# A fixed order for TensorE and the transfer queue in the opening of a one-layer decoder kernel

## The chip, the cores and the metric

The kernel runs on one core of one Trainium2 chip. The metric is the device time of one execution in microseconds (us); lower is better. Three runs of the kernel before took 2656.65, 2659.69 and 2660.51 us, with a median of 2659.69. All arithmetic is in float32.

## What is computed

A decoder layer on `x` of shape (4, 2048, 512). Three branches are each applied to a layer norm and added back to `x`:

```python
x = x + attn(_layernorm(x))          # a recurrence along the first axis (4 steps), 8 blocks of 64 states
x = x + xattn(_layernorm(x), ctx)    # 16 heads over 77 context rows
x = x + ffn(_layernorm(x))

# attn: z <- V (A z + u_t), output 2 Re z
# xattn: softmax(Q K^T / sqrt(32)) V, then Wo
# ffn:
h = einsum('bsd,dh->bsh', x, W_exp) + b_exp      # 512 -> 2048
h = butterfly(h, up_weights, 2048)               # 11 stages of 2x2 mixes
h = gelu(h + up_bias)
h = butterfly(h, down_weights, 2048)
y = einsum('bsh,hd->bsd', h, W_con) + b_con      # 2048 -> 512
```

The recurrence runs over only 4 steps, so it equals four 64 x 64 coefficient matrices. A butterfly is a linear map, so each of the two can be multiplied into the matrix beside it once, before any token is touched.

## The kernel before, in words

The program has an opening and sixteen equal units. A unit takes 128 positions of all four rows of the first axis. For unit u, `front` makes the recurrence, the norms and the cross attention, and `feed_forward` the third branch; `feed_forward(u)` draws `front(u + 1)` forward step by step, so that the two are mixed on TensorE. Products of two by two blocks use seven multiplications in place of eight (`seven`, and the seven matrices `up7`, `dn7`, `wq7`).

The opening prepares what the units need:

- `_recurrence_taps` (L68): the coefficients `gt`. A chain of small VectorE operations (L54 to L107), then four rounds of small products on TensorE (`ps_g` L111 and L112, `ps_rr` and `ps_ri` L121 to L124), each of which needs the VectorE results of the round before (L127 to L130).
- `_keys_values` (L134): loads the context and two weight matrices, then four groups of key products (L145), whose results are copied into the block-diagonal `kbd` by VectorE (L149), and four of value products (L154).
- `_prepare` (L218): multiplies the butterflies into the weights. For the first one: coefficient products on GpSimd (L179, L204), a bias product (L267), products over the low stages (L276), transposes (L285), products over the high stages against diagonals `bd` that VectorE makes (L242, L298, with the bias in L303), then for each of eight blocks four sums (L317 to L320, GpSimd and VectorE in turn) and stores to `up7`. For the second one: coefficient products on GpSimd (L179 on `low_dn`), products over the high stages (L333), transposes (L343), products over the low stages (L352), sums (L363 to L366) and stores to `dn7`.
- `front(0)`: the first unit's own front, with transposes L468 and L439, recurrence products L498, q products L483 (`ps_q`), scores L541, softmax L545 to L551, L563 to L575 and the output product L483 (`ps_w`).

These four are Python generators or plain calls; the code of L757 to L805 draws them forward. `next(prep)` issues the instructions up to the next `yield`. The order in which the code is written is however not the order on the chip: a scheduler that assigns the instructions to their engines reorders each engine's instructions by priority and by what is ready in its own estimate, except those held with `keep_in_program_order`. Each engine then takes its instructions strictly in the order so fixed, with semaphores between the engines. All transfers are issued by SP, one queue. Tiles come from pools with tags; a tile waits for a buffer of its tag to be free. The PSUM tag "f" has two buffers and serves the front and the recurrence; "a", "b" and "c" have two each and serve `_prepare`, keys and values.

In the opening's order before, the recurrence's products come between those of L276, keys and values come after the four groups of L298, and `front(0)` is mixed in from L468 on. The eight blocks of sums run beside keys and values. The last steps before unit 0's `feed_forward` are the seven `ps_w` products, a norm (L404 to L417, L430), the transposes L439, and then the first `ps_a` of L642, which needs the tile `w_up` that L651 loads. The tile `db` (L804), a bias, takes a buffer with the tag "xn", the one of the normalised rows of L430.

Of the kernel before, what the change touches and what calls it, by code (L numbers as in the profile page):

```python
# [17 lines left out]
P = 128  # L18
# [49 lines left out]
def _recurrence_taps(nc, pool, psum, ssm_vec, ssm_vt, ssm_vinv, gt):  # L68
# [40 lines left out]
    for j in range(T):  # L109
# [3 lines left out]
        for h in range(2):  # L113
            if j + h < T:
                q = slice(h * NS, (h + 1) * NS)
                nc.vector.tensor_scalar(gt[q, j + h, :], ps[q, 0:NS], 2.0, None, ALU.mult)
        if j == T - 1:
            break
# [15 lines left out]
def _keys_values(nc, psum, ctx_t, wk_t, wv_t, kbd, vsb, room):  # L134
# [82 lines left out]

def _prepare(nc, keep, pool, sums, room, banks, dram, ident, wexp_t, up_low, up_high, up_bias, dn_low, dn_high, wcon, wup, wdn, bias,  # L218
             up7, dn7):
# [19 lines left out]

    def diagonal(hp, m):  # L240
        bd = pool.tile([P, NB, sub], F32, tag="bd", bufs=4, name="bd")
        keep(nc.vector.tensor_tensor(bd, hp[:, m, :].unsqueeze(2).to_broadcast([P, NB, sub]),  # L242
                                     mask.unsqueeze(1).to_broadcast([P, NB, sub]), ALU.mult))
        return bd.rearrange("p b i -> p (b i)")
# [24 lines left out]
    nc.sync.dma_start(out=bias, in_=up_bias)  # L269
    mid = wup.rearrange("p c (m k) -> p c m k", m=NB)  # L270
    for g in range(4):
# [21 lines left out]
    for g in range(4):  # L293
        bd = [diagonal(hp, 4 * g + j) for j in range(4)]
        for c in range(NC):
# [78 lines left out]
def kernel(ctx: ExitStack, tc: tile.TileContext, x, ctx_t, ssm_vec, ssm_vt, ssm_vinv, wq_t, wk_t, wv_t,  # L374
# [381 lines left out]
    ready = []  # L756
    with ExitStack() as stack:  # L757
        pool = stack.enter_context(tc.tile_pool(name="prep", bufs=1))
        wup = pool.tile([P, NC, HID], F32, name="wup")
        wdn = pool.tile([P, NB, D], F32, name="wdn")  # L760
        with tc.tile_pool(name="taps", bufs=1) as taps:
            _recurrence_taps(nc, taps, psum, ssm_vec, ssm_vt, ssm_vinv, gt)
        sums = stack.enter_context(tc.tile_pool(name="sums", bufs=2))
        high = work.tile([P, 2, HIGH, NB // 2, 4], F32, tag="xn", name="high")
        prep = _prepare(nc, tc.keep_in_program_order, pool, sums, high, banks, dram, ident, wexp_t, up_low, up_high, up_bias, dn_low, dn_high, wcon,
                        wup, wdn, hbias, up7, dn7)
        next(prep)
        xts[0] = load_x(0)
        room = (work.tile([P, NC, T * NK], F32, tag="pr", name="ct"), xpool.tile([P, NC, D], F32, tag="xt1", name="wk"),
                work.tile([P, NC, D], F32, tag="qt", bufs=1, name="wv"))  # L770
        keys = _keys_values(nc, psum, ctx_t, wk_t, wv_t, kbd, vsb, room)
        next(keys)
        for _ in range(5):
            next(prep)
        wq = work.tile([P, 7, NC // 2, D // 2], F32, tag="pt", bufs=1, name="wq")
        first = front(0, xts.pop(0), ready, wq)
        for n, _ in enumerate(prep):
            for _ in range(1 + (n > 8)):
                next(first, None)
            if n == 7:  # L780
                next(keys)
                src = wq_t.rearrange("(c p) e -> p c e", p=P)
                for i, (c, e) in ((0, (0, 0)), (1, (1, 0)), (3, (1, 1)), (6, (0, 1))):
                    nc.sync.dma_start(out=wq[:, i], in_=src[:, 2 * c : 2 * c + 2, e * (D // 2) : (e + 1) * (D // 2)])
                tc.keep_in_program_order(nc.gpsimd.tensor_tensor(wq[:, 4], wq[:, 6], wq[:, 3], ALU.add))
                nc.gpsimd.tensor_tensor(wq[:, 6], wq[:, 0], wq[:, 6], ALU.subtract)
                nc.gpsimd.tensor_tensor(wq[:, 5], wq[:, 4], wq[:, 0], ALU.subtract)
                nc.gpsimd.tensor_tensor(wq[:, 2], wq[:, 1], wq[:, 5], ALU.subtract)
            if n == 9:
                nc.sync.dma_start(out=wq7, in_=wq)  # L790
            if n == 11:
                src = wo_t.rearrange("(c p) e -> p c e", p=P)
# [91 lines left out]
```

## Time and profile before

| | us |
|---|---|
| median of three runs | 2659.69 |
| the profiled execution | 2664.3 |
| its span, first to last instruction | 2662.5 |
| TensorE busy over the span | 2583.4 (97%) |
| VectorE, ScalarE, GpSimd busy | 1463.9, 807.3, 949.9 |
| TensorE busy in 0 to 249 us | 195.15 |
| first product of L642 starts | 248.96 |

A line of the timeline gives the start and the length in us, the engine, the line of the program, the operation, the tile written and those read, the shape, and how many instructions were merged into it; in brackets, the idle time before it and what ended that. A float32 product appears as two records. The line numbers are those of the kernel before; those of the same statement in the changed kernel are a few higher (seven from `front` on).

### The profile page before, as it was taken

The numbers are of one execution on the slowest core, as the hardware profiler recorded it, in microseconds if no ns is written. First come the engines' busy times: TensorE is split into PE (matmuls) and PEld (weight loads), VectorE is DVE, ScalarE is ACT, GpSimd is POOL, SyncE is SP. The second block draws the span as 40 slices with busy tenths as digits, with TensorE's granted clock in tenths as the row PEclk, the third lists the DMA queues.
The fourth block names the chain that finished last, engine by engine and source line by source line (L and its number), as shares of the span: only waits on it lengthen the run. The fifth ranks groups of instructions, "written<-read, shape, count | busy, mean of one in ns | idle before, by whom it ended". The sixth has DMA issues, their size and how long they took to land.

```text
span 2662.5 us, 37405 instructions
## 1 busy us (share of the span) xinstructions
PE 2583.4 (97%) x14536; PEld 2196.8 (83%) x14536; DVE 1463.9 (55%) x3350; ACT 807.3 (30%) x1466; POOL 949.9 (36%) x1023
## 2 busy tenths in 40 slices
PE   7887999999999999999999999999999999999999
PEld 6665888888888888888888888888888888888888
DVE  5567554556455455546555555655555564554541
ACT  2132413324141332414133241413234141423420
POOL 3323251523434152333415243341524234252523
PEclk9998999999999999999999999999999999999999
DMA  7704324242332424233342424333242423323243
GB/s 211 237 19 167 131 86 148 96 167 95 123 131 102 148 80 172 94 129 121 105 145 97 155 94 155 111 105 131 97 161 88 161 101 114 136 98 137 95 130 140
DMA packets 94656, 333.60 MB, mean 125 GB/s; under 512 B 17424, under 2 KB 46224, under 8 KB 77328
## 3 DMA queue, kind: packets, MB, share of 16 engines
q1 hardware_dynamic: 94480, 331.21, 35.7%
q8 instruction: 116, 1.90, 0.3%
q14 instruction: 60, 0.49, 0.1%
HBM read 297.61 MB, written 33.57 MB: 124 GB/s over the span
## 4 chain that ended last, share of the span: by engine, by line
PE 86%; DVE 7%; ACT 5%; issue 2%; POOL 0%; DMA 0%; SPq 0%; ACTq 0%; DVEq 0%; POOLq 0%
PE ps_a L709 13%; PE ps_b L642 10%; PE ps_b L709 8%; PE ps_q L483 7%; PE ps_w L483 7%; PE ps_c L642 7%; PE ps_a L642 7%; PE ps_c L709 6%; PE ps_sc L541 5%; PE ps_pt L563 4%; PE ps_s L498 3%; PE ps_o L573 2%; PE ps_t L439 2%; ACT L547 1%; ACT L647 1%
## 5 line engine op out<-in xcount | busy, mean ns | idle before, releaser
L642 PE MATMUL ps_b<-tb,w_up 128*128 128x256 f32 x1536 | 396.8, 379 | 1.2 <-DVE u L659 1.2
L709 PE MATMUL ps_a<-w_dn,a 128*128 128x256 f32 x1536 | 373.0, 380 | 0.0
L685 POOL TENSOR_TENSOR s<-a,a 128x256 f32<-128x256 f32 x128 | 92.7, 724 | 670.3 <-ACT a L647 447.9
L642 PEld LDWEIGHTS ps_b<-tb,w_up 128*128 128x128 f32 x1536 | 287.0, 190 | 40.9 <-issue 1.6
L647 ACT ACTIVATE a<-a,hbias 128x256 f32<-128x256 f32 x384 | 193.6, 508 | 410.9 <-DVE a L680 278.5
L709 PEld LDWEIGHTS ps_a<-w_dn,a 128*128 128x128 f32 x1536 | 282.4, 190 | 41.6 <-issue 3.0
L642 PE MATMUL ps_a<-xnt,w_up 128*128 128x256 f32 x1024 | 263.9, 381 | 0.0
L709 PE MATMUL ps_c<-w_dn,s 128*128 128x256 f32 x1024 | 248.6, 379 | 0.0
L551 POOL TENSOR_TENSOR pr<-pr,sm 128x1232 f32<-128x1232 f32 x64 | 143.9, 2248 | 288.8 <-DVE sm L550 241.0
L440 ACT COPY xnt<-ps_t 128x512 f32<-128x512 f32 x128 | 73.5, 586 | 550.7 <-PE ps_t L439 550.7
L642 PEld LDWEIGHTS ps_a<-xnt,w_up 128*128 128x128 f32 x1024 | 192.0, 191 | 25.7
L709 PEld LDWEIGHTS ps_c<-w_dn,s 128*128 128x128 f32 x1024 | 188.7, 190 | 27.8
L591 DVE TENSOR_TENSOR xt<-ps_w,xt 128x512 f32<-128x512 f32 x96 | 66.2, 689 | 215.0 <-PE ps_w L483 148.5
L697 POOL TENSOR_TENSOR xt<-xt,ybias 128x256 f32<-128x256 f32 x128 | 99.5, 811 | 223.2 <-DVE xn L430 223.2
L541 PE MATMUL ps_sc<-kbd,qt 128*128 128x308 f32 x512 | 173.5, 435 | 3.7 <-DVE pr L546 2.1
L483 PE MATMUL ps_q<-xnt,wq 128*128 128x256 f32 x640 | 152.4, 381 | 0.7 <-ACT qt L523 0.7
L563 PEld LDWEIGHTS ps_pt<-ident,pr 128*77 128x77 f32 x1024 | 117.9, 147 | 40.6 <-ACT a L647 11.0
L563 PE MATMUL ps_pt<-ident,pr 128*77 128x128 f32 x1024 | 143.8, 276 | 5.5 <-ACT a L647 4.7
L547 ACT ACTIVATE pr<-pr 128x308 f32<-128x308 f32 x256 | 111.5, 457 | 118.5 <-DVE pr L546 117.9
L483 PEld LDWEIGHTS ps_q<-xnt,wq 128*128 128x128 f32 x640 | 122.1, 191 | 17.9 <-ACT qt L523 1.1
L642 PE MATMUL ps_c<-tb,w_up 128*128 128x256 f32 x512 | 131.6, 379 | 0.0
L642 PE MATMUL ps_c<-xnt,w_up 128*128 128x256 f32 x512 | 131.5, 379 | 0.0
(199 smaller groups left out, 4550.8 us busy)
## 6 DMA issues: line engine op xcount, KB each, us to landing
w_up<-up SPq DMA_DIRECT2D x128, 896.0 KB, 4.5
w_dn<-dn SPq DMA_DIRECT2D x112, 1024.0 KB, 4.8
wq<-wq SPq DMA_DIRECT2D x16, 1792.0 KB, 8.5
xt<-in_x SPq DMA_DIRECT2D x16, 1024.0 KB, 5.4
out<-xt SPq DMA_DIRECT2D x64, 256.0 KB, 4.8
wdn<-in_wexp_t SPq DMA_DIRECT2D x4, 1024.0 KB, 11.3
wdn<-in_wcon SPq DMA_DIRECT2D x4, 1024.0 KB, 5.9
up<-s SPq DMA_DIRECT2D x8, 512.0 KB, 3.3
```

The lines of the kernel that those rows point to most:

```text
L440: nc.scalar.copy(xnt[:, :, t, :], ps)
L483: nc.tensor.matmul(tiles[key][:, r, :], lhsT=lhs(i, r, k), rhs=rhs(i, r, k), start=key == i and r == 0 and k == 0, stop=k == 1, skip_group ...
L498: nc.tensor.matmul(ps[:, 2 * i : T, f * NS : (f + 1) * NS], lhsT=xpt[:, i, c * (P // NS) + f, :], rhs=gt[:, 0 : T - 2 * i, :], start=i == ...
L541: nc.tensor.matmul(ps[:, 0 : 4 * NK], lhsT=qt[:, g, t, :], rhs=kbd[:, t, g, :], start=True, stop=True)
L547: nc.scalar.activation(pg, pg, AF.Exp, scale=1.0 / math.sqrt(DH))
L551: nc.gpsimd.tensor_tensor(pr, pr, sm.unsqueeze(2).to_broadcast([P, NH, NK]), ALU.mult)
L563: nc.tensor.transpose(pt_ps[0:NK, j, :], pr[:, 4 * g + j, :], ident)
L642: nc.tensor.matmul(ps, lhsT=w[:, c, :], rhs=rhs[i - 1][:, c], start=first and c == 0, stop=c == 1, skip_group_check=True)
L647: nc.scalar.activation(out, x, AF.Gelu, bias=hbias[:, b : b + 1])
L685: nc.gpsimd.tensor_tensor(s1, a21, a22, ALU.add)
L697: nc.gpsimd.tensor_tensor(r, r, ybias[:, d], ALU.add)
L709: nc.tensor.matmul(ps[:, t, :], lhsT=act[p][lhs[i]][:, t, :], rhs=w[:, p, :], start=first and p == 0 and t == 0, stop=p == h - 1, skip_gro ...
```

## The change

In the opening the order of TensorE and of SP is no longer left to the scheduler: under `manual_schedule` they take their instructions as the code writes them. VectorE, ScalarE and GpSimd are still scheduled. The code that draws the generators forward is rewritten: the recurrence now yields after each round, keys and values after each group, and the steps are interleaved by the list of `run` calls. By it the load of x comes first; keys and values stand between the recurrence's rounds; the first half of `front(0)` comes before L276; the high coefficients are loaded ahead of the low ones; q, scores and softmax stand between the groups of L298 and the sums, `ps_w` between the steps of L343 and L352; the second unit's x (`load_x(1)`) is loaded last. To that end the sums and the diagonals use the tiles of `wo`, `ybias` and a new `more` as room in place of pool buffers, the weights `wcon` are loaded by quarters after each group of L298, and the bias product takes the bias as its stationary operand, with one row as its result.

```diff
@@ _recurrence_taps
                 nc.vector.tensor_scalar(gt[q, j + h, :], ps[q, 0:NS], 2.0, None, ALU.mult)
+        yield
         if j == T - 1:
             break
@@ _keys_values
     for g in range(NC):
-        ps = psum.tile([P, 512], F32, tag="a", name="ps_k")
+        ps = psum.tile([P, 512], F32, tag="ab"[g % 2], name="ps_k")
...
                                   ps[q, 0 : T * NK].rearrange("p (b k) -> p b k", b=T))
+        yield
     for b in range(T):
-        ps = psum.tile([P, 512], F32, tag="b", name="ps_v")
+        ps = psum.tile([P, 512], F32, tag="c", name="ps_v")
...
         nc.scalar.copy(vsb[:, b, :], ps[0:NK, :])
-    yield
+        yield
@@ _prepare
-    def diagonal(hp, m):
-        bd = pool.tile([P, NB, sub], F32, tag="bd", bufs=4, name="bd")
+    def diagonal(hp, m, place):
+        bd = place.rearrange("p (b i) -> p b i", b=NB)
...
+    brw = room2
+    for high, coefs in zip(highs, (up_high, dn_high)):
+        nc.sync.dma_start(out=high, in_=coefs)
...
-    for high, coefs in zip(highs, (up_high, dn_high)):
-        nc.sync.dma_start(out=high, in_=coefs)
     yield
...
-    ps = banks()
-    for b in range(NB):
-        nc.tensor.matmul(ps[:, b : b + 1], lhsT=e[:, b, :], rhs=b1[:, b : b + 1], start=True, stop=True)
-    nc.vector.tensor_copy(b1, ps[:, 0:NB])
+    for g in range(4):
+        ps = banks()
+        for j in range(4):
+            b = 4 * g + j
+            nc.tensor.matmul(ps[0:1, j * P : (j + 1) * P], lhsT=b1[:, b : b + 1], rhs=e[:, b, :], start=j == 0, stop=True,
+                             skip_group_check=True)
+        nc.scalar.copy(brw[:, g, :], ps[0:1, :])
...
-    nc.sync.dma_start(out=brow[0, :].rearrange("(b p) -> p b", p=P), in_=b1)
+    nc.sync.dma_start(out=brow[0:1, :], in_=brw.rearrange("o g x -> o (g x)"))
...
-        bd = [diagonal(hp, 4 * g + j) for j in range(4)]
+        bd = [diagonal(hp, 4 * g + j, room3[:, (4 * g + j) * P : (4 * g + j + 1) * P]) for j in range(4)]
...
+        nc.sync.dma_start(out=t[:, 4 * g : 4 * g + 4, :], in_=wcon.rearrange("(p m) d -> p m d", m=NB)[:, 4 * g : 4 * g + 4, :])
         yield
...
-    src = wcon.rearrange("(p m) d -> p m d", m=NB)
-    for i in range(4):
-        nc.sync.dma_start(out=t[:, 4 * i : 4 * i + 4, :], in_=src[:, 4 * i : 4 * i + 4, :])
...
-        s = sums.tile([P, 4, k, P], F32, name="s")
+        s = room3[:, p % 3 * 1024 : p % 3 * 1024 + 1024].rearrange("p (i k q) -> p i k q", i=4, k=k)
...
+    more = sums[0].tile([P, 8, P], F32, name="more")
+    places = [more[:, i] for i in range(8)] + [room4[:, i * P : (i + 1) * P] for i in range(4)]
+    places += places[0:4]
...
-        bd = [diagonal(hp_dn, 4 * g + j) for j in range(4)]
+        bd = [diagonal(hp_dn, 4 * g + j, places[4 * g + j]) for j in range(4)]
@@ tile_decoder_kernel
-    with ExitStack() as stack:
+    E = mybir.EngineType
+    with ExitStack() as stack, tc.manual_schedule(engines={E.PE, E.SP}):
...
-        with tc.tile_pool(name="taps", bufs=1) as taps:
-            _recurrence_taps(nc, taps, psum, ssm_vec, ssm_vt, ssm_vinv, gt)
-        sums = stack.enter_context(tc.tile_pool(name="sums", bufs=2))
...
-        next(prep)
-        xts[0] = load_x(0)
...
-        next(keys)
-        for _ in range(5):
-            next(prep)
...
-        first = front(0, xts.pop(0), ready, wq)
+        with tc.tile_pool(name="taps", bufs=1) as tp:
+            taps = _recurrence_taps(nc, tp, psum, ssm_vec, ssm_vt, ssm_vinv, gt)
+            xts[0] = load_x(0)
+            first = front(0, xts.pop(0), ready, wq)
+
+            def run(*gens):
+                for g in gens:
+                    next(g, None)
+
+            run(taps, keys, prep)
+            src = wq_t.rearrange("(c p) e -> p c e", p=P)
+            for i, (c, e) in ((0, (0, 0)), (1, (1, 0)), (3, (1, 1)), (6, (0, 1))):
+                nc.sync.dma_start(out=wq[:, i], in_=src[:, 2 * c : 2 * c + 2, e * (D // 2) : (e + 1) * (D // 2)])
+            run(first, keys, keys, taps, keys, keys, taps, keys, keys, taps, taps)
+        sums.append(stack.enter_context(tc.tile_pool(name="sums", bufs=1)))
+        run(first, keys, first, keys, first, first, prep, first, first, first, first)
+        nc.gpsimd.tensor_tensor(wq[:, 4], wq[:, 6], wq[:, 3], ALU.add)
...
+        run(prep, prep, first, prep, first, first, prep, first, first)
+        run(prep, prep, prep, prep)
+        run(first, first, first, prep, first, first, prep, first, first, prep, first, first, prep)
+        nc.sync.dma_start(out=wq7, in_=wq)
         for n, _ in enumerate(prep):
-            for _ in range(1 + (n > 8)):
+            for _ in range(1 + (n < 4)):
                 next(first, None)
-            if n == 7:
-                next(keys)
...
-            if n == 11:
+            if n == 4:
                 src = wo_t.rearrange("(c p) e -> p c e", p=P)
...
-                xts[1] = load_x(1)
+        xts[1] = load_x(1)
         for _ in first:
             pass
```

The order that results was read from both built programs. On TensorE it is, in the changed kernel: `ps_g`; 8 keys; `ps_rr`, `ps_ri`, `ps_g`; 8 keys; the same round; 8 values; the same round; 4 values; 4 transposes; 4 values; 12 transposes; all of L498; the bias; L276 with L439 in its last third; L285; q steps in pairs between the four groups of L298, with the first four scores before the fourth; four scores; then L563, L573 and scores for one row of the first axis after another, with the groups of L333 between them from the last scores on; then L343 and L352 with a `ps_w` step after every second; two of L352; the last transposes; L642. On SP it is as the code reads; the last part is the stores to `dn7`, then the loads `xt1`, `ybias`, `db`, and then the first `w_up`.

More of the change, by code (lines that the diff above doesn't have):

```diff
@@ L215, in _regrouped, with _prepare @@
     return out
-def _prepare(nc, keep, pool, sums, room, banks, dram, ident, wexp_t, up_low, up_high, up_bias, dn_low, dn_high, wcon, wup, wdn, bias,
+def _prepare(nc, keep, pool, sums, room, room2, room3, room4, banks, dram, ident, wexp_t, up_low, up_high, up_bias, dn_low, dn_high, wcon, wup, wdn, bias,
              up7, dn7):
@@ L760 @@
         wdn = pool.tile([P, NB, D], F32, name="wdn")
-        with tc.tile_pool(name="taps", bufs=1) as taps:
-            _recurrence_taps(nc, taps, psum, ssm_vec, ssm_vt, ssm_vinv, gt)
-        sums = stack.enter_context(tc.tile_pool(name="sums", bufs=2))
         high = work.tile([P, 2, HIGH, NB // 2, 4], F32, tag="xn", name="high")
-        prep = _prepare(nc, tc.keep_in_program_order, pool, sums, high, banks, dram, ident, wexp_t, up_low, up_high, up_bias, dn_low, dn_high, wcon,
-                        wup, wdn, hbias, up7, dn7)
-        next(prep)
-        xts[0] = load_x(0)
+        row = work.tile([1, 4, 4 * P], F32, tag="pr", name="row")
+        sums = []
+        prep = _prepare(nc, tc.keep_in_program_order, pool, sums, high, row, wo.rearrange("p i k d -> p (i k d)"), ybias, banks, dram, ident, wexp_t, up_low, up_high,
+                        up_bias, dn_low, dn_high, wcon, wup, wdn, hbias, up7, dn7)
         room = (work.tile([P, NC, T * NK], F32, tag="pr", name="ct"), xpool.tile([P, NC, D], F32, tag="xt1", name="wk"),
@@ new lines @@
+        sums.append(stack.enter_context(tc.tile_pool(name="sums", bufs=1)))
+        run(first, keys, first, keys, first, first, prep, first, first, first, first)
+        nc.gpsimd.tensor_tensor(wq[:, 4], wq[:, 6], wq[:, 3], ALU.add)
+        nc.gpsimd.tensor_tensor(wq[:, 6], wq[:, 0], wq[:, 6], ALU.subtract)
+        nc.gpsimd.tensor_tensor(wq[:, 5], wq[:, 4], wq[:, 0], ALU.subtract)
+        nc.gpsimd.tensor_tensor(wq[:, 2], wq[:, 1], wq[:, 5], ALU.subtract)
+        run(prep, prep, first, prep, first, first, prep, first, first)
@@ L777 @@
+        run(prep, prep, prep, prep)
+        run(first, first, first, prep, first, first, prep, first, first, prep, first, first, prep)
+        nc.sync.dma_start(out=wq7, in_=wq)
         for n, _ in enumerate(prep):
-            for _ in range(1 + (n > 8)):
+            for _ in range(1 + (n < 4)):
                 next(first, None)
-            if n == 7:
-                next(keys)
[L782 to L788, printed above, removed]
@@ L789 @@
-            if n == 9:
-                nc.sync.dma_start(out=wq7, in_=wq)
-            if n == 11:
+            if n == 4:
                 src = wo_t.rearrange("(c p) e -> p c e", p=P)
```

## The prediction

> **What bounds the kernel now.** I read the page first, for the share of each engine and its forty slices; then the busy time by stage; then the timeline of each engine over the first 260 us; last, the two orders of instructions, engine by engine.
>
> ```profile
> PE   7887999999999999999999999999999999999999
> PEclk9998999999999999999999999999999999999999
> ```
>
> Forty slices of 66.6 us. Only the first four of TensorE are below 9: what can change lies in the opening. The stages say the same (the columns: length, busy time with instructions of PE, PEld, DVE, ACT and POOL, granted clock, DMA share, GB/s):
>
> ```profile
> 0.00:249.00 249.00, 195.15 (x1129) 153.09 (x1130) 157.71 (x352) 61.66 (x103) 81.28 (x122) 0.93 0.51 165
> 400.00:550.00 150.00, 148.67 (x846) 127.00 (x845) 82.36 (x195) 47.79 (x87) 53.34 (x56) 1.00 0.35 125
> ```
>
> After 249 us TensorE is busy 148.67 of 150. From there on both kernels issue the same instructions in the same order, but for a handful at the seam. So the time moves with one number: when the first ps_a of L642 starts, 248.96 now.
>
> Of the 195 us of TensorE in the opening some 160 would do. I add the groups at the rate of their fast rows: recurrence 3.5, bias 3.5, L276 14.4, L285 7.2, transposes 2.0+1.8+1.8, L298 14.9 with L303 3.8, L498 5.6, keys 8.6, values 13.9, q 12.1, L333 14.9, scores 8.2, L563 7.0, L573 4.0, L343 7.0, L352 13.7, w 12.1. The rest is half rate:
>
> ```profile
> 42.90 2.93 PE L276 MATMUL ps_p<-low_up,wdn 128*128 128x128 f32 x12
> ...
> 47.91 8.75 PE L276 MATMUL ps_p<-low_up,wdn 128*128 128x128 f32 x76
> ...
> 245.40 3.76 PE L439 MATMUL ps_t<-ident,xn 128*128 128x128 f32 x16 [7.78 <-DVE xn L430]
> 248.96 3.10 PE L642 MATMUL ps_a<-xnt,w_up 128*128 128x256 f32 x8
> ```
>
> One L276 row is 0.244 us before 47 us and 0.115 after; a transpose after a wait of 7.78 is 0.235, elsewhere 0.11. (The granted clock of the page reads 9 in the first slice all the same; I go by the rows.) With 54 us of waits this makes the 89 us that could be won at the very most.
>
> **The new order, stage by stage.** Line numbers are those of before. I lay the durations of before's rows along the new order; each engine takes its instructions strictly in turn.
>
> *Start, 12.9 (now 8.35).* x is issued ahead of the recurrence's inputs: 0.74 + the 5.4 that an xt load takes = 6.1. VectorE then has four BATCH_NORM_STATS2 (1.26 for two, 2.5) among the exponential's chain (L55 to L107, 5.13 to 8.29: 3.2) and some 1.1 of the norm's small steps.
>
> *To 61: recurrence, keys, values, front.* ps_g 1.0; eight key products 4.3 at full rate, 8.2 at half (22.1); ps_rr and ps_ri 1.1. VectorE now has eight kbd copies (3.91 for 8) ahead of L127 to L130 (1.3), so TensorE waits to 25.2. Again 0.7 + 4.3 + 1.1 and a wait of 1.9: 33.2. Values 6.9, recurrence 1.8, wait 1.4: 43.3; 0.7 + 6.9 + 0.4: 51.3; twelve transposes with evictions 2.5, L498 5.7: 59.5. For a clock that falls back in those waits I add 1.5 (bounds 0 and 6: half rate for none, or for all of the second key octet and a little more). Keys and values hide nothing now (89.47 to 112.41); here they fill the recurrence's waits, and this is the gain.
>
> *To 88.6: the up butterfly.* Bias 3.5 (it becomes sixteen products of one column of weights, nowhere in the trace: between 1.8 at a transpose's 0.11 and 7.0, which L267 takes at half rate; I take the 0.22 of one L276 product, which streams as many columns), L276 14.4, transposes 1.8, L285 7.5, 0.5 wait. The weights are in by about 38: 11.3 MB at the 299 to 377 GB/s of 8 to 28 us.
>
> *To 127: q between L298.* q 12.1, three groups of 4.7, the copy of xnt and L513 to L515 2.3 beyond the first q step, and 1.0 before each of three groups, since the diagonals (L242) queue on VectorE behind L520. Before the fourth they queue behind a whole softmax: 6.9. Sum 38.4.
>
> *To 168.9: the sums.* Here nothing covers. Only 16.7 us of TensorE stand between the fourth L298 group and the first L333: the group itself, three times scores, two times L563 and L573. VectorE has three softmax rounds of 8 x 0.48 + 1.42 + 0.24 (16.5), sixteen sums at 0.41 to 0.93 (9.6), four pt and two ot copies (4.2): 30.3. Ahead are the group and its eviction 4.4 and GpSimd's first sums 2.9 (L319 three times, 0.72, before the first L317), and 4.3 go on GpSimd's L551 (2.25) and on L573. Total 41.9. In before these sums lie beside keys and values.
>
> *To 237.4: the down butterfly.* The diagonals of L333 meet GpSimd's long operations. Uncovered, four take 0.89; beside L179 they took 6.68:
>
> ```profile
> 132.19 9.38 POOL L179 TENSOR_TENSOR low_dn<-low_dn 128x64 f32<-128x64 f32 x6
> ...
> 135.04 6.68 DVE L242 TENSOR_TENSOR bd<-hp_dn,mask 128x128 f32<-128x128 f32 x4
> ...
> 148.94 0.89 DVE L242 TENSOR_TENSOR bd<-hp_dn,mask 128x128 f32<-128x128 f32 x4
> ```
>
> In the new order group 0's stand beside L551 (2.7, as the 2.88 of 168.08), group 1's beside the sums of wo (3.5), group 3's beside sw (3.0), group 2's free (0.5): 9.7; all free they would be 3.1, all as slow as the worst row 26.7. L333: the first group at half rate after the empty stretch 6.5, three at 3.73; two rounds of L563, L573 and copies 7.0; then L343, L352 and the seven w steps, now interleaved, 32.8, and 1.3 of evictions. Sum 68.5. The last w step stands 1.9 before that, at 235.5; now it ends at 237.6 (235.73 + 1.89). The whole new order is worth 2 us at this point.
>
> *Edits at nothing.* The wcon loads now go out after each L298 group, the last near 132: 5.9 to landing, wanted at 169. wo's tile now holds the sums' three buffers and the first diagonals, so its load waits for the last up store: near 170, plus 4.2 and 5.8 of GpSimd's sums makes 180, wanted at 211; without that cover each us late is a us. The tile xp comes into the buffer that the high coefficients free, behind GpSimd's products for both butterflies and wq's sums, near 46; its transposes stand at 51. If the loads came 6 us later this wait would show. low_dn's load (8.7) now goes out near 78 with b2's behind it: 88, wanted at 94.
>
> *The tail.* Now 11.3 us pass from the last w step to L642. Then:
>
> ```profile
> 226.48 0.81 SPq L651 DMA_DIRECT2D w_up<-up  x2
> 227.34 0.43 SPq L396 DMA_DIRECT2D xt<-in_x  x1
> 227.81 0.93 SPq L651 DMA_DIRECT2D w_up<-up  x1
> 248.34 0.33 SPq L804 DMA_DIRECT2D db<-in_down_bias  x1
> ```
>
> L804's tile takes the buffer of a normalised row, so it waits for the third group of transposes, 2.9 after the first transpose (245.40 to 248.34). Now w_up has gone 20 us before. In the new order SP's queue is fixed as written: dn7, xt1, ybias, db, and only then the first w_up (dn7's last transfer used to be issued by 222.3 and w_up 4.2 later; that, too, has moved behind the last L352). So: last w step to first transpose 11.5 (L591 0.69, two BATCH_NORM_STATS2 1.3, two evictions' copies and aggregates 1.2, L363, L365 and L366 some 5.3 as in the rows of 215 to 221, the norm's thirteen steps 2.45, L430 0.5); 2.9 to db's issue; 0.4 for it and 0.4 for w_up's; 4.5 to landing. 19.7 against 11.3: **8.4 lost**. Behind the waiting db stand w_up 0 to 2 and xt2, and for w_up waits L642, hence everything. Bounds: 4.4 if the norm's chain is free of L363 to L366, 13 if w_up also waits for xt1 (5.4).
>
> L642 starts at 235.5 + 19.7 = 255.2, 6.2 later. TensorE has waited 5 us more just before and starts at half rate for another 1.5. In sum +7.7. The profiled execution took 2664.3 (span 2662.5 and 1.8 around it); it becomes 2672.0. Against the median of the three runs, 2659.69, I forecast **2667**.
>
> **Two rules of the Trainium skill.** On the clock the rows come first: half rate follows waits of 3.2 to 7.8 us and then lasts 5 to 6.5 us (224.93 to 230, 245.40 to 252); but from 20.8 to 47 it lasts although TensorE is shown busy without a gap. "TensorE: Matmul & The Clock Gate", Part 1, says that about 3.4 us of sustained work restore the full rate and one idle window of that length takes it away. The trace agrees on the idle side and not on the opening. By the rule the first key octet would lose 1.7 and L333 1.7, 3.3 us less than in my sum. "SBUF — State Buffer", section "SBUF: two separate sides", says that a VectorE operation with two SBUF inputs and a GpSimd operation lock each other out for a whole instruction. The 6.68 against 0.89 agrees, and it speaks against this change, which lays L333's diagonals beside GpSimd's products.
>
> **Rivals.**
> 1. *Faster, about 2648.* For it: keys and values, 23 us that now run bare, do fill the recurrence's waits. Every term at its kinder end: keys at full rate but for 1.7 (-2.2), no clock allowance (-1.5), diagonals free (-6.6), L333 at full rate (-2.8), sums at 0.41 (-3), tail at 4.4 (-4): 20.1 less than +7.7. Against: the rows of contention.
> 2. *The same, about 2660.* VectorE, not TensorE, sets the pace: it has 158 us of work in the opening and keeps its order. The change would then only move where TensorE waits; the tail's loss and keys' gain cancel. For it: the stretch to 168.9 is VectorE's alone.
> 3. *Much slower, about 2684.* The clock stays at half rate until 61 as it did until 47 under the recurrence's small products: second octet +4.3, values +13.7, less the 1.5 allowed and what hides: +17. It decides if the small products between the octets hold the clock down. Against: octets of 4 to 8 us without a gap.
> 4. That the order doesn't come out as written is excluded: the listed order shows it.
>
> **Chances.** Forecast's neighbourhood (2665 to 2680) 0.40, rival 3 0.14, rival 2 0.16, rival 1 0.30. A measurement of this kernel can tell about 0.2% (5.3 us) from no change: faster 0.30, same 0.16, slower 0.54. The range takes in most of rivals 1 and 3: 2645 to 2688. The slower case's own: 2664 to 2682.
>
> **What would show it.** First ps_g near 13; L298's first group near 90; a stretch of some 38 us from 131 with TensorE a third busy and VectorE full; the diagonals of L333 at several us for four; w_up's first issue after db, some 15 us after the last w step; L642 near 255. Wrong I would be if VectorE's copies between the recurrence's steps don't hold TensorE, or if w_up's landing isn't what L642 waits for.

## The result, and the profile after

The changed kernel is slower: median 2682.68 us of four runs (2681.00 to 2684.32) against 2659.69 of four runs of the kernel before (2656.65 to 2660.51). The ratio is 1.0089, with a 95% interval of 1.0071 to 1.0106; that is 23 us. Its profiled execution took 2681.39 us with a span of 2679.6, 17.1 us more than that of before.

From here on the line numbers are those of the kernel named; in the changed kernel L642 is L649, L651 is L658, L439 is L446, L333 is L340, L242 is L244, L298 is L304, L363 to L366 are L370 to L373. First the slices of the changed kernel's page:

```profile
PE   7876999999999999999999999999999999999999
PEclk9978999999999999999999999999999999999999
```

Again only the first four slices have digits below 9. The stages of the changed kernel (columns as before: length, busy time of PE, PEld, DVE, ACT and POOL, clock, DMA share, GB/s), up to the first L649 and in the steady state:

```profile
0.00:266.00 266.00, 196.99 (x1129) 151.14 (x1130) 150.01 (x349) 65.13 (x108) 85.35 (x127) 0.86 0.45 148
416.00:566.00 150.00, 148.67 (x846) 127.12 (x845) 82.33 (x194) 47.49 (x87) 53.08 (x56) 1.00 0.36 125
```

The steady state is the same to the hundredth (148.67 of 150). TensorE is busy 196.99 until the first L649 instead of 195.15, and idle 69.0 instead of 53.9: nearly all of what the change cost is idle time (15.1 of 16.9 us). Which idle time, TensorE's timeline of the changed kernel tells:

```profile
23.70 6.10 PE L146 MATMUL ps_k<-ct,wk 128*128 128x308 f32 x16
...
103.77 3.84 PE L304 MATMUL ps_p<-wo,wdn 128*128 128x128 f32 x32 [0.98 <-DVE wo L244]
...
126.44 0.71 PE L304 MATMUL ps_p<-wo,wdn 128*128 128x128 f32 x4 [3.48 <-DVE wo L244]
128.89 5.94 PE L304 MATMUL ps_p<-wo,wdn 128*128 128x128 f32 x28 [1.74 <-DVE wo L244]
...
170.77 1.22 PE L340 MATMUL ps_p<-more,wdn 128*128 128x128 f32 x4 [3.48 <-DVE more L244]
173.22 5.96 PE L340 MATMUL ps_p<-more,wdn 128*128 128x128 f32 x28 [1.23 <-DVE more L244]
...
187.66 5.36 PE L340 MATMUL ps_p<-more,wdn 128*128 128x128 f32 x26 [0.25 <-DVE more L244]
192.87 3.83 PE L340 MATMUL ps_p<-ybias,wdn 128*128 128x128 f32 x32
...
204.18 5.85 PE L340 MATMUL ps_p<-more,wdn 128*128 128x128 f32 x28 [0.48 <-DVE more L244]
...
253.19 3.76 PE L446 MATMUL ps_t<-ident,xn 128*128 128x128 f32 x16 [9.56 <-DVE xn L437]
265.69 2.05 PE L649 MATMUL ps_a<-xnt,w_up 128*128 128x256 f32 x4 [8.74 <-DMA w_up<-up]
```

Two things are to be seen. Where TensorE waits for the diagonals several times close together, the group behind runs at half rate (28 records in 5.96 or 5.85, while the group without a wait takes 3.83 for 32); the second and third L304 groups, behind one wait of about 1 us each, do not (3.84, as at 103.77, and 3.81). And the first L649 starts at 265.69 instead of 248.96 (+16.7), after a wait of 8.74 that the kernel before doesn't have. Added up over the timeline until 275, TensorE's waits by what ended them, in us:

| waits of TensorE for | before | changed |
|---|---|---|
| the diagonals (`bd`; `wo` and `more` of L244) | 7.6 | 18.2 |
| w_up's load | 0 | 8.7 |
| the normalised rows `xn` | 15.0 | 9.6 |
| softmax (`pr`) | 2.1 | 8.0 |
| the recurrence (start, `gt`, `ti`) | 16.0 | 17.0 |
| all, with those not listed | 54.9 | 68.7 |

And the end of the opening on SP's queue of the changed kernel, start and length of each group of issues:

```profile
243.98 2.01 SPq L375 DMA_DIRECT2D dn<-wdn  x3
247.78 3.81 SPq L375 DMA_DIRECT2D dn<-wup  x4
251.64 1.28 SPq L403 DMA_DIRECT2D xt<-in_x  x1
253.01 1.29 SPq L817 DMA_DIRECT2D ybias<-in_b_con  x1
256.13 0.34 SPq L818 DMA_DIRECT2D db<-in_down_bias  x1
256.97 0.80 SPq L658 DMA_DIRECT2D w_up<-up  x2
```

dn7's second half leaves 29 us later than before (its last issue ended at 222.31 there), and w_up goes out behind it all, at 256.97 instead of 226.48.

### The profile page after: what moved, and what is told of

Same layout as the page of the kernel before. It is cut to its first block, busy times and chain, and to the rows that moved or that the text cites. A ratio compares the mean times of both kernels' runs of the same rounds, so it can differ in the third digit from the quotient of the medians.

```text
span 2679.6 us, 37402 instructions
## 1 busy us (share of the span) xinstructions
PE 2586.2 (97%) x14536; PEld 2197.8 (82%) x14536; DVE 1454.6 (54%) x3349; ACT 810.2 (30%) x1470; POOL 947.8 (35%) x1023
## 4 chain that ended last, share of the span: by engine, by line
PE 82%; DVE 6%; ACT 4%; issue 1%; DMA 1%; SPq 0%; ACTq 0%; DVEq 0%
PE ps_a L716 12%; PE ps_b L649 10%; PE ps_b L716 8%; PE ps_w L490 7%; PE ps_a L649 7%; PE ps_c L649 7%; PE ps_q L490 7%; PE ps_c L716 6%; PE ps_sc L548 4%; PE ps_pt L570 4%; PE ps_s L505 3%; PE ps_o L580 2%; PE ps_t L446 2%; ACT L554 1%; ACT L654 1%; DVE st L411 1%
## 5 line engine op out<-in xcount | busy, mean ns | idle before, releaser
L649 PE MATMUL ps_b<-tb,w_up 128*128 128x256 f32 x1536 | 397.8, 380 | 0.0
L649 PEld LDWEIGHTS ps_b<-tb,w_up 128*128 128x128 f32 x1536 | 288.0, 191 | 39.3 <-issue 0.2
L649 PE MATMUL ps_a<-xnt,w_up 128*128 128x256 f32 x1024 | 263.9, 380 | 8.7 <-DMA w_up<-up 8.7
L649 PEld LDWEIGHTS ps_a<-xnt,w_up 128*128 128x128 f32 x1024 | 191.9, 191 | 34.5 <-POOL ybias L819 9.1
L704 POOL TENSOR_TENSOR xt<-xt,ybias 128x256 f32<-128x256 f32 x128 | 99.2, 807 | 223.3 <-DVE xn L437 223.2
L490 PE MATMUL ps_q<-xnt,wq 128*128 128x256 f32 x640 | 151.3, 380 | 0.0
L490 PEld LDWEIGHTS ps_q<-xnt,wq 128*128 128x128 f32 x640 | 121.4, 190 | 16.2
L649 PE MATMUL ps_c<-tb,w_up 128*128 128x256 f32 x512 | 132.3, 381 | 0.0
L649 PE MATMUL ps_c<-xnt,w_up 128*128 128x256 f32 x512 | 131.5, 379 | 0.0
```

The lines of the kernel that those rows point to most:

```text
L490: nc.tensor.matmul(tiles[key][:, r, :], lhsT=lhs(i, r, k), rhs=rhs(i, r, k), start=key == i and r == 0 and k == 0, stop=k == 1, skip_group ...
L649: nc.tensor.matmul(ps, lhsT=w[:, c, :], rhs=rhs[i - 1][:, c], start=first and c == 0, stop=c == 1, skip_group_check=True)
L704: nc.gpsimd.tensor_tensor(r, r, ybias[:, d], ALU.add)
```

## The experiments

Each was timed beside the kernel before, in 5 to 12 runs (the changed kernel in four). Theory 1 is that the tail (what lies between the last w step and the first up product) is the price, theory 2 the diagonals' place on VectorE, theory 3 that keys and values are missed as cover in the later stages. "Last w step" is the end of the last L490.

| kernel | median us | ratio to before (95%) |
|---|---|---|
| changed | 2682.7 | 1.0089 (1.0071 to 1.0106) |
| w steps last | 2681.1 | 1.0079 (1.0065 to 1.0093) |
| db free | 2681.7 | 1.0083 (1.0069 to 1.0096) |
| both of these | 2676.8 | 1.0066 (1.0050 to 1.0081) |
| xt1 early | 2679.9 | 1.0076 (1.0063 to 1.0090) |
| diagonals ahead | 2654.1 | 0.9977 (0.9965 to 0.9989) |
| keys and values late | 2676.6 | 1.0057 (1.0038 to 1.0076) |
| ahead, other tail | 2654.7 | 0.9976 (0.9965 to 0.9988) |
| ahead, other tail, xt1 early | 2651.8 | 0.9966 (0.9951 to 0.9981) |
| ahead in the up butterfly | 2671.0 | 1.0038 (1.0026 to 1.0050) |
| ahead in the down butterfly | 2665.0 | 1.0015 (1.0004 to 1.0026) |
| ahead, keys and values late | 2661.7 | 1.0003 (0.9991 to 1.0015) |
| kernel before, diagonals ahead | 2639.1 | 0.9918 (0.9906 to 0.9931) |

### The tail: four edits

```diff
@@ w steps last
-            for _ in range(1 + (n < 4)):
+            for _ in range((1 + (n < 4)) * (n < 9)):
@@ db free
-        db = work.tile([P, D], F32, tag="xn", name="db")
+        db = work.tile([P, D], F32, tag="pr", name="db")
@@ xt1 early: xts[1] = load_x(1) moved behind wo's sums (n == 4)
```

> The changed kernel with one order altered: the seven w steps (L490) no longer stand between the pairs of L350 and L359 but behind all of them; dn7's second half then goes out some 12 us sooner, and the sums L370 to L373 leave the norm's chain. Theory 1 (the tail is the price: norm chain 11.3 instead of 7.8, db's issue 2.9, w_up's landing 8.7 instead of 4.6): the last w step stays near 242 to 243, then 7.8 + 2.9 + 0.8 + 4.6 to the first L649, near 259 instead of 265.7; time about 7 us below the changed kernel, near 2676. Rival (without work between them the w steps pay their own waits, 19.7 us for the seven in the kernel before against 12.1 of busy time): the last w step goes to 249, the gain is eaten up, time within 2 us of the changed kernel.

> The changed kernel with db in another buffer (tag pr), so that its load need not wait for the third group of transposes. Theory 1 (w_up stands in SP's queue behind the waiting db): db's issue goes from 256.1 to 254.4, w_up's from 257.0 to 254.8, the first L649 some 2 to 3 us sooner, time 2679 to 2681. Rival (the transfer engines are 0.96 busy from 243.6 to 265.7, dn7's second half, xt1, the two biases and w_up going through one after the other, so w_up lands when the bytes are through): the issue goes forward, the landing does not, first L649 within 1 us of 265.7, time as the changed kernel.

> Both edits together: w steps last, and db in a buffer of its own. Theory 1: w_up is there before the norm is done, nothing but the norm's chain and four groups of transposes lie between the last w step and the first L649: 7.8 + 3.6, so near 254 instead of 265.7; time 12 us below the changed kernel, near 2671; that is the whole loss of the tail, and 4 to 8 us stay above the kernel before for the rest of the opening. Rival (w steps without cover): 2676 to 2680.

> The changed kernel with xt1's load issued behind wo's (near 172) instead of behind dn7's last transfer; ybias and db stay where they are. Theory 1 (the issue of w_up waits for db's, which waits for the transposes; then its landing is 8.7 because 1 MB of xt1 and the biases are ahead): the issue stays at 256 to 257, the landing comes down to 5 or 6, first L649 near 262.5, time 3 us below the changed kernel. Rival (dn7's stores alone hold the transfer engines until 256): no change within 1 us.

**db free** is the plainest. SP's queue of that kernel:

```profile
248.10 3.80 SPq L375 DMA_DIRECT2D dn<-wup  x4
...
254.64 0.63 SPq L818 DMA_DIRECT2D db<-in_down_bias  x1
257.31 0.81 SPq L658 DMA_DIRECT2D w_up<-up  x2
```

db goes out sooner, w_up doesn't: it waits on, and the first L649 starts at 265.42. So the rival was right that freeing db gains nothing, though not in its reason: it had the issue go forward and the landing wait for bytes in the queue, and the issue itself waits. For what, the distance from the end of dn7's last issue to w_up's issue tells: 5.4 us here, 5.4 in the changed kernel, 5.7 with the w steps last, 5.9 with xt1 early, 4.2 in the kernel before. The profile names dn7's stores (`dn<-wup`) as what ended L658's wait: 1.8 us of waiting here, 2.1 with both edits, 2.8 with the w steps last. So w_up starts when these stores have landed; it takes memory that the opening's weights give back. In the changed kernel the profile puts 0.3 us on them, behind db: there db and the stores come free almost together, and freeing db alone could not gain more.

**w steps last** brought w_up's issue to 244.20 and **both** to 244.47, as theory 1 wanted, and the first L649 to 258.6 and 258.9 (theory 1 had 259 and 254); but instead of the 7 and 12 us expected the median fell by 1.6, which the intervals do not separate from nothing, and by 5.9. Rows of the run with both, from TensorE, GpSimd and VectorE, and last a row of TensorE with the w steps last:

```profile
239.50 6.49 PE L490 MATMUL ps_w<-wo,sw 128*128 128x256 f32 x16 [3.25 <-DVE xt L598]
...
255.16 1.94 PE L446 MATMUL ps_t<-ident,xn 128*128 128x128 f32 x8 [5.71 <-DVE xn L437]
```

```profile
234.37 5.66 POOL L603 TENSOR_TENSOR xt<-xt,w 128x512 f32<-128x512 f32 x3
```

```profile
232.30 3.19 DVE L372 TENSOR_TENSOR wup<-wdn,wup 128x1024 f32<-128x1024 f32 x1
235.53 2.17 DVE L373 TENSOR_TENSOR wup<-wdn,wup 128x1024 f32<-128x1024 f32 x1
```

```profile
267.83 1.18 PE L649 MATMUL ps_b<-tb,w_up 128*128 128x256 f32 x4 [3.86 <-DVE u L666]
```

The wait of 9.56 for `xn` falls to 5.71, but dn7's sums on VectorE now meet L603 on GpSimd (5.66 instead of 3.71, L372 3.19 instead of 1.23), the w steps wait for both, run at half rate (16 records in 6.49) and end at 249.4 instead of 241.9. That is where the rival had the last w step, by another way than it said. Nor is all of what the first L649 gains kept: with the w steps last its products wait 0.54, 0.68 and 3.86 us for `tb` and `u`, and the next unit's first transpose (L475) comes at 272.18, only 2.2 us sooner than in the changed kernel (274.38); with both it comes at 269.28, 5.1 sooner. **xt1 early** changed nothing in w_up's issue (256.76), but the load landed after 6.7 us instead of 8.6. The next unit's transposes were drawn into the gap, the first L649 even stands later behind them (268.50), and a fixed point further on, the first w_dn product, came 1.3 us sooner. The median is 2.8 us lower, about theory 1's number, but the intervals of the two ratios do not separate it from nothing.

### The diagonals

```diff
+    ups = [diagonal(hp, m, room3[:, m * P : (m + 1) * P]) for m in range(NB)]
     for g in range(4):
-        bd = [diagonal(hp, 4 * g + j, room3[:, (4 * g + j) * P : (4 * g + j + 1) * P]) for j in range(4)]
+        bd = ups[4 * g : 4 * g + 4]
...
+        if g == 0:      # more and places are made here, no longer behind L181
+            downs = [diagonal(hp_dn, m, places[m]) for m in range(12)]
...
     for g in range(4):                                   # the L340 groups
-        bd = [diagonal(hp_dn, 4 * g + j, places[4 * g + j]) for j in range(4)]
+        bd = downs[4 * g : 4 * g + 4]
...
+        if g == 0:
+            downs += [diagonal(hp_dn, m, places[m]) for m in range(12, 16)]
```

> The changed kernel with the diagonals (L244) written ahead on VectorE: all sixteen of the up butterfly before its first L304 group, twelve of the down butterfly behind the first L304 group, the last four behind the first L340 group. The same operations, only earlier in VectorE's order. Theory 2 (the waits of TensorE before L304 and L340 come from the place of the diagonals, behind a softmax or beside GpSimd's products): 8.3 us of waits before L304 and 9.9 before L340 go, and some of the half rate behind them; the first L340 near 163, the last w step near 230, time 10 to 15 us below the changed kernel, 2667 to 2672. Rival (rival 2 of the prediction: VectorE's work sets the pace, so TensorE only waits elsewhere): the sums' stretch gets longer by what is saved, time within 4 us of the changed kernel. If only L340's part comes through: near 2675.

> Diagonals ahead in the up butterfly only: all sixteen before the first L304 group; the down butterfly's stay where the change has them. Of the run with both (first L340 12.2 us sooner, last L359 25.5 us sooner, time 28 us lower) this should give the first part. If the two parts are independent: first L340 near 159 to 160, its waits of 9.9 us unchanged, time 10 to 13 us below the changed kernel, 2670 to 2673. Rival (the later part only pays because the earlier one makes room): more or less than that by over 5 us.

> Diagonals ahead in the down butterfly only: twelve behind the first L304 group, four behind the first L340 group; the up butterfly's stay. Independent parts: the waits of 8.3 us before L304 unchanged, first L340 at 167 to 171, L350 begins near 196 instead of 209.9, time 13 to 16 us below the changed kernel, 2667 to 2670. If only the waits of 9.9 us are worth something and not the half rate behind them: near 2673.

2654.1: 28.6 us below the changed kernel, twice what theory 2 expected, and 6 below the kernel before. TensorE in the run with both parts, the fourth group of the up butterfly and the four of the down butterfly (L305, L343 there):

```profile
120.73 3.73 PE L305 MATMUL ps_p<-wo,wdn 128*128 128x128 f32 x32
...
158.56 5.49 PE L343 MATMUL ps_p<-more,wdn 128*128 128x128 f32 x32
...
169.06 3.84 PE L343 MATMUL ps_p<-more,wdn 128*128 128x128 f32 x32
172.74 3.74 PE L343 MATMUL ps_p<-ybias,wdn 128*128 128x128 f32 x32
...
180.30 3.84 PE L343 MATMUL ps_p<-more,wdn 128*128 128x128 f32 x32
```

Not one of them waits (the first L305 group still does, 1.05 us, and runs slow, as does the first L343 group behind the waits of the scores). VectorE makes all 28 diagonals between 92.7 and 101.2, in 5.90 us for 28, in a stretch where it has time. The sums' stretch that follows, from the end of the up butterfly's products to the first L343, got no longer (125.1 to 158.6, 33.5; 135.5 to 170.8, 35.3, in the changed kernel), so the rival that VectorE's work sets the pace falls. Until the first up product (238.86) TensorE is busy 186.88 and idle 52.1: of 27 us, 16.9 are waits, and 10.1 are less busy time for the same products, which now run less often at half rate. The expectation had only "some of the half rate" for that second part.

The two parts add up: the up butterfly's alone gives 11.7 (first L340 at 162.2, with waits there nearly as in the changed kernel), the down butterfly's 17.7 (L350 from 190.8 instead of 209.9, a little more than expected), both 28.6.

### Keys and values

The load of wv goes to two other buffers (the end of wo's memory and ybias); four key groups stand between q and L304, the values around the fourth L304 group, in `run(first, first, first, keys, prep, first, keys, first, prep, keys, first, keys, first, prep, first, first, keys, keys, keys, prep, keys)`; in the run with the diagonals ahead the last two entries change places, and four of the down butterfly's diagonals are made only after the fourth L304 group. The recurrence has `run(first, taps, taps, taps, taps)`.

> The changed kernel with keys and values not in the recurrence but later: the four key groups between q and L304, the values around the fourth L304 group (wv in two other buffers, so one load more). Theory 3 (keys and values were cover in the kernel before, and the loss is that the later stages have none): the recurrence ends some 20 us sooner, the waits of 8.3 us before L304 and some of 5 behind it are filled, first L340 near 163 to 167, time 4 to 8 us below the changed kernel. Rival (they fill the recurrence's waits as well there as later ones, and without them TensorE waits for x's load, the weights and GpSimd's products until about 45): first L340 170 to 176, time as the changed kernel or up to 6 us above it.

> Diagonals ahead, and keys and values late (between q and L304 and ahead of the fourth L304 group, wv in two other buffers; four of the diagonals one stage later). With the diagonals behind, the late place made no difference to the opening (first L340 at 170.0 against 170.8). The prediction's step was that in the recurrence they fill waits, and that this is the gain. If that is so, the late place now costs what they fill there: the recurrence is done 14 us sooner, 22.5 us of products come back later with no wait left for them to fill: 6 to 9 us above the run with the diagonals ahead, 2660 to 2664. Rival (they keep TensorE at full rate in the sums' stretch, whatever the diagonals do): within 4 us of 2654.

With the diagonals in their late place, keys and values late are a gain: 2676.6, 6 us below the changed kernel in the median, as theory 3 expected. The fourth L304 group, behind the values, no longer waits (128.02, at full rate). The profiled execution, the longest of the six, has only 1.2 of it in its span and the first L340 at 170.0, as the rival said; where the others gained more no trace tells. With the diagonals ahead the same move costs 7.6 (2661.7 against 2654.1), as expected. So keys and values do fill the recurrence's waits, and that is worth some 8 us once the diagonals are made in time; as long as the later stages wait for diagonals, keys and values fill those waits at least as well. Theory 3 is right only that far. In the run with the diagonals ahead the recurrence without keys and values shows what they also do, its small products and the first group behind them:

```profile
25.40 0.69 PE L111 MATMUL ps_g<-vt,pz_next 64*128 64x64 f32 x2 [1.07 <-DVE ti L130]
...
36.58 6.77 PE L515 MATMUL ps_s<-gt,xpt 128*128 128x256 f32 x32
```

At half rate still (0.69 for two records at 25 us; L515, with 6.77, in part); with the octets between, the changed kernel had 0.43 for such a pair from 20 us on, and 5.40 for the group.

### Both together, and the kernel before

The kernels "other tail" have the diagonals ahead, three w steps between the first pairs of L350 and L359 and four behind the last (`n < 12` in the edit above), and db free.

> Diagonals ahead, and a tail of its own: three w steps between the first pairs of L350 and L359, so that GpSimd's L603 is done early, four behind the last pair; db in a buffer of its own. Theory 1: with L370 to L373 out of the norm's chain and dn7 gone some 7 us sooner, the last w step to the first L649 takes 11 to 13 us instead of 23.8, 8 us more than what the run with the diagonals alone gains; theories 1 and 2 together near 2660, level with the kernel before. Rival (VectorE's sums L370 to L373 now hold the four w steps' additions): 4 us of that at most.

> As the run before with xt1's load issued behind wo's as well, so that the second unit's statistics no longer stand in the first unit's up products (VectorE's steps of 0.65 beside GpSimd's additions, before the first u) and 1 MB less goes out behind dn7. Theory 1: another 1 to 3 us, near 2658. Rival (nothing waits for xt1): no difference from the run without it.

The other tail brought the first up product forward by 7.5 us (231.36 against 238.86), and the time by nothing (2654.7; the rival had allowed 4 us at most). Eight products later TensorE waits:

```profile
231.36 2.04 PE L654 MATMUL ps_a<-xnt,w_up 128*128 128x256 f32 x4 [3.41 <-POOL tb L625]
...
241.94 2.05 PE L654 MATMUL ps_b<-tb,w_up 128*128 128x256 f32 x4 [5.34 <-DVE u L671]
```

VectorE does the next unit's norm there, in steps of 0.65 beside GpSimd's L709 that take 0.16 elsewhere, and u stands behind it. With xt1 early that norm is done sooner, and the time falls to 2651.8: the miss is partly made good, and the expectation of another 1 to 3 us held.

For the kernel before, the diagonals were put into wo's memory (sixteen, then twelve behind the first L298 group, four behind the first L333 group) and wo's load behind L333.

> The kernel before with its diagonals written ahead (in wo's memory, wo's own load later for it). There TensorE waits 7.6 us for diagonals in four places, with some half rate behind them. Theory 2 (the price is VectorE's order, which the fixed order makes worse: 18.2 us of such waits in the changed kernel): 5 to 11 us below the kernel before, 2649 to 2655, about level with the changed kernel with the diagonals ahead; the fixed order itself then gives next to nothing. Rival (the kernel before loses nothing there, because other work is moved into the place): within 3 us of 2660, and the fixed order with the diagonals ahead is a gain of 6.

2639.1, 22 us below the kernel before: the fastest of all, and twice the most that theory 2 gave it; the rival, that nothing was to be had there, falls. That is more than its 7.6 us of waits for diagonals: the edit also moves wo's load and lets the scheduler reorder the rest, and how much of the 22 is which was not separated. TensorE of the kernel before with the diagonals ahead:

```profile
114.26 9.10 PE L336 MATMUL ps_p<-wo,wdn 128*128 128x128 f32 x80
123.58 1.11 PE L444 MATMUL ps_t<-ident,xn 128*128 128x128 f32 x8 [0.22 <-DVE xn L435]
...
219.99 3.76 PE L444 MATMUL ps_t<-ident,xn 128*128 128x128 f32 x16 [7.78 <-DVE xn L435]
223.54 2.80 PE L647 MATMUL ps_a<-xnt,w_up 128*128 128x256 f32 x8
```

Where it had waited 7.19 us for the first norm (at 121.07), there now stand two and a half of the four groups of the down butterfly (80 records of 128): with their diagonals made, the scheduler could draw them forward. Idle time until the first up product falls from 53.9 to 39.0, busy time from 195.15 to 184.50.

## Why the prediction was right in sign and too small in size

The sign held: the fixed order gains in the recurrence and gives it back later, above all in the tail. The size was 7.7 for 17.1 in the profiled execution (23 in the medians). At the last w step the ledger had the new order 2 us ahead; it was 4.3 behind (241.9 against 237.6). For the tail it had 8.4 lost; it was 12.4. Step by step, the ledger's time against the measured one:

| until | ledger | measured | difference so far |
|---|---|---|---|
| first ps_g | 12.9 | 11.8 | -1.1 |
| end of L505 (59.5, with 1.5 for the clock 61) | 61 | 58.2 | -2.8 |
| q begins | 88.6 | 85.1 | -3.5 |
| fourth L304 group | 127 | 126.4 | -0.6 |
| first L340 | 168.9 | 170.8 | +1.9 |
| end of the last L359 | 237.4 | 243.6 | +6.2 |
| first L649 | 255.2 | 265.7 | +10.5 |

- **Start, recurrence, front, up butterfly: right**, 3.5 us too dear. Keys and values fill the waits (2.03, 2.03 and 1.07 remain); the run with the diagonals ahead puts their place at 7.6 us. Rival 3 fell: the first octet brings TensorE to full rate by 20 us (0.38 for a ps_rr pair), and the values keep it (7.09 for 16 records). But its mechanism is there: behind the wait of 2.03 the second octet took 6.10 instead of 4.31, 1.8 us, so the allowance of 1.5 was needed. What was too dear is the start (11.8), the first octet (7.04 for 8.2) and the front.
- **Luck.** These 3.5 us hid part of what came later: from q on the ledger was 14.0 us short, 2.9 until the fourth L304 group, 2.5 in the sums, 4.3 in the down butterfly, 4.3 behind it. And 2682.7 lies next to rival 3's 2684, but rival 3's slow clock in the recurrence gave only the 1.8 us above.
- **q and sums: each right within 3 us**, but I took the diagonals' places as given costs (1.0 three times, 6.9 before the fourth group), and half rate behind them for nothing.
- **Down butterfly: the half rate was mis-sized.** With 9.7 for the diagonals and 6.5 for one group at half rate the stage came to 68.5; it took 72.9. TensorE's waits for diagonals within it were 6.4, less than the 9.7 (another 3.5 stand before its first product). But three groups ran slow, not one: without the waits the four took 24.6 instead of 17.7. Rival 1's kind end put 6.6 on these diagonals and 2.8 on the half rate; the run with these diagonals ahead gave 17.7.
- **The tail: the step with the wrong cause.** It said "Behind the waiting db stand w_up 0 to 2 and xt2, and for w_up waits L642", and took 0.4 and 4.5 from db's issue to landing. db's issue came as said (2.9 behind the first transpose), and w_up's 15.1 behind the last w step, as said too; but freeing db moved nothing, since w_up's load waits for dn7's stores as well, whose sums stand behind the last L359. The prediction had the 4.2 us from dn7's last transfer to w_up in the kernel before, and made no wait of it; that its time for the issue came out is luck. The term that was mis-sized is the landing: 8.7, not 4.5. From 243.6 to 265.7 the transfer engines were busy 0.96 of the time at 319 GB/s, with those stores, xt1 and the biases, and with xt1 out of the way the landing took 6.7; that the rest comes from the stores and the biases is argued, not shown. Tail 23.8 instead of 19.7, against 11.3 before.
- **Rival 2, VectorE's pace: false.** The same work in another order took 28.6 us less.

What of the 23 us is what, by the ratios to the kernel before (0.0089, 23.7 us of 2660): with the diagonals ahead in both kernels, 0.9977 against 0.9918, the fixed order is still 0.0059 or 15.7 us behind (each ratio is known to some 0.0012 to 0.0018, so these shares are good to a few us). The traces have 15.3 of that at the first up product: 11.2 are the tail (22.5 against 11.3 from the last w step on), 3.9 the start (12.19 against 8.34, x ahead of the recurrence's inputs). The other 0.0030, 8 us, are the diagonals: making them ahead gained 0.0082 (21.8 us) before, with all that the scheduler then moved, and 0.0112 (29.8 us) in the fixed order. The tail was not won back: of four edits the best two together gave 5.9, and whether a place for w_up outside the memory of the opening's weights gives the rest was not tried.

## What to carry to other kernels

When a fixed order is written, write out the small operations that feed TensorE too, and early: an operation of 0.2 us that stands behind a softmax on its engine costs its wait and can cost the half rate of the group behind. Ask of every load between two stages not only what is ahead of it in the queue but whose memory it takes; the stores that must land first can be the wait even when the queue is free. And judge a gain at a fixed point some way behind the place that was changed: the first product came forward by 7.5 us once without the time moving.

## What the runs showed of the hardware that was not expected

- After waits of 3.5 and 1.2 us one on the other the next group ran at half rate through all its 28 records (5.96 us). Groups behind three smaller waits close together did so too (1.84, 0.78 and 0.25 before 187.66; 1.01, 0.80 and 0.48 before 204.18); behind a single wait of about 1 us the group at 103.77 did not (3.84). Over 1 us at a time the record of the granted clock agrees: 0.50 from 186 to 192 and from 203 to 209. In the second octet it is 0.50 from 25.2 to 28.4. Over the whole opening it was 0.93 in the kernel before (to 249), 0.86 in the changed kernel (to 266) and 0.95 in the fastest kernel (to 223.5).
- "TensorE: Matmul & The Clock Gate", Part 1, of the Trainium skill, says that some 3.4 us of sustained work give the full rate. In the changed kernel full rate stood at the latest 7 us after the first key product. In the run with the diagonals ahead and keys and values late, with small products and gaps of 0.45 to 1.58 us between them, it had not come by 25.4 us, 13 us after the first product (0.69 for a pair).
- GpSimd beside VectorE: L603 5.66 for three instead of 3.71, VectorE's norm steps of 0.16 in 0.65 beside L704, one VectorE sum of 1.23 in 3.19. The page "SBUF — State Buffer" of the Trainium skill, section "SBUF: two separate sides", says that a VectorE operation with two inputs in SBUF and a GpSimd operation that reads SBUF keep each other out for a whole instruction. These rows agree, and here steps of four elements a row are held too.
